# A four-layer graph network: the dilation's comparison on 2-byte operands in pairs of batches

## The chip, the cores and the metric

The kernel runs on one core of a Trainium2 chip. The metric is the device time of one execution in microseconds; the time of a kernel is the median of several executions. The engines are named as in the profile: PE is the matrix engine (PEld its weight loads), DVE the vector engine, ACT the scalar engine, POOL the GpSimd engine, SP the sync engine, which here only issues DMAs. `L1096` is line 1096 of the kernel before. The kernel is written against a layer that takes tiles and operations, inserts all waits, and orders each engine's instructions with a scheduler; each engine then executes its own instructions in that order.

## The reference

There are 16 batches of a graph of 1024 nodes with 128 features, and an adjacency matrix `adj` per batch, symmetric, of zeros and ones, with about 6% ones and a full diagonal. Four layers follow, each as `x = layernorm(x + layer(x, adj))`: an attention layer with a gate (0), a three-step neighbour aggregation on a *dilated* adjacency (1), a second attention layer with three gates (2), and a graph convolution (3). The change concerns the dilation alone, which comes ahead of layer 1:

```python
def step(carry, n):                       # n = 0 .. 1023, one row after the other
    row = jnp.take(carry, n, axis=0)
    nbi = row.astype(jnp.int32)
    num = jnp.sum(nbi)
    sf = jnp.where(num > T_DIL, (num + K_DIL - 1) // K_DIL, 1)   # T_DIL = 10, K_DIL = 2
    rank = jnp.cumsum(nbi)
    rm = row & (rank % sf == 0)
    valid = (mask_b[n] != 0) & (num > 1)
    rm = jnp.where(valid, rm, False)
    keep = ~rm
    carry = carry.at[n].set(row & keep)
    carry = carry.at[:, n].set(carry[:, n] & keep)
    return (carry, None)
...
adj_d = adj * jax.vmap(_dilate_pattern)(adj > 0, mask)
```

Each row loses the neighbours whose rank is a multiple of half of the row's count (that is, about the middle one and the last one), and the same entries are taken out of the column. Later rows see the removals of earlier ones.

## The kernel before, in words

The adjacency of all 16 batches lies in SBUF as FP8, in tiles `carry` (in the code `Y[b]`, 128 partitions by 8 blocks by 1024). Layer 0 fills them. Then comes the dilation, then layer 1, which reads the dilated matrices, and last a joint section for layers 2 and 3, which reads the undilated ones back from DRAM.

The dilation works on blocks of 128 rows (`k` = 0 to 7) and on two groups `g` of eight batches (`GB` = 8). A pair (k, g) is called a step here; there are 16, numbered 0 to 15 in the order k first, then g. One step has three parts.

`prepare` computes, for the 128 rows of the block, the rank of each member inside the diagonal block by matmuls against triangular matrices (L1068), once for each four batches (`QB` = 4). DVE masks the block (`uY`, L1062), multiplies ranks and mask into `sk` (L1070: 128 partitions by 8 batches by 128 members, fp16), and derives per row the count of members (`l1`, L1071) and a check (`past`, L1074). In the last two blocks (k = 6 and 7) it also marks the last member (`last`, L1076).

`fixed_point` finds which members of the diagonal block fall out. A row's middle rank depends on how many members earlier rows of the same block have taken from it, and so the kernel iterates: from a guess `ti` (128x8, int32) a threshold `thr` is made by setting the lowest bit (L1091); in blocks 6 and 7 also `even` (L1094); then `mid` = (`sk` == `thr`) over 128x1024 elements (L1096, FP8 result), whose ones are the middle members; PE counts them per row with eight matmuls, one for each batch, with a batch's 128x128 part of `mid` as weights and a column of ones as the moving operand (`pd`, L1099; in blocks 6 and 7 eight more with `last`, L1101); and DVE adds the count to the base `v1m` to give the next `ti` (L1103). Each turn of this loop is called an evaluation. Their number is fixed per block:

```python
EVALS = 2, 3, 4, 7, 7, 3, 3, 9
```

The last `mid` of a step is removed from the block's FP8 bits by XOR on 32-bit words (L1112), after `last` was added to it in blocks 6 and 7 (L1108, L1109). Then some ten small operations on 128x8 elements give the three values that the removals need: `negc`, `posc` and, as the last one, `wid` (L1129).

`removal` does the rest of the rows' width, one batch at a time. PE makes ranks of all 1024 columns (`s`, L1141 and L1143), ACT turns them into distances from the middle (`q`, L1144, two halves), DVE compares the distance with `wid` (`keep`, L1147) and masks the rows (L1148), PE transposes the result and adds it (`pc`, L1151 to L1155), and ACT writes the block's column (`carry`, L1156). In the last block each finished batch of the first half is also stored to DRAM (L1158).

The steps are woven as follows. Loop i (1 to 16) takes in turns the fixed point of step i and the eight removals of step i-1, and after each four removals one half of the `prepare` of step i+1. So a removal of step i waits for the `wid` of step i, and a fixed point waits for its own `prepare`, which reads what the removals before it left. The turns are only the order in which the program is written down; the scheduler orders the instructions of each engine from there. Ahead of loop 1, the fixed point of step 0 runs beside the end of layer 0 for the last batch, and a power on POOL (`deg`, L1187) is placed there too.

The tiles `sk`, `mid`, `uY`, `q` and `keep` have two buffers each.

Of the kernel before, what the change touches and what calls it, by code (L numbers as in the profile page):

```python
# [10 lines left out]
F16 = mybir.dt.float16  # L11
F32R = mybir.dt.float32r
BF16 = mybir.dt.bfloat16
I32 = mybir.dt.int32
I8 = mybir.dt.int8
FP8 = mybir.dt.float8e4
AF = mybir.ActivationFunctionType
OP = mybir.AluOpType
# [4 lines left out]
P = 128  # L23
# [4 lines left out]
EVALS = 2, 3, 4, 7, 7, 3, 3, 9  # L28
GB = 8
QB = 4  # L30
# [3 lines left out]
def general_kernel(ctx: ExitStack, tc: tile.TileContext, t: dict, out: bass.AP):  # L34
# [155 lines left out]
    with tc.tile_pool(name="m_sb", bufs=1) as sb, tc.tile_pool(name="m_ps", bufs=1, space=PSUM) as ps:  # L190
        mi = sb.tile([BT, P], I32, name="mi")
        nc.sync.dma_start(mi, t["nodemask"].rearrange("b (t p) -> (b t) p", p=P))
# [10 lines left out]
    carry_pool = carry_ctx.enter_context(tc.tile_pool(name="carry", bufs=1))  # L203
    C = [carry_pool.tile([P, NT, N], I8, name=f"carry{b}") for b in range(B)]

# [82 lines left out]
    with ExitStack() as ph:  # L288
# [15 lines left out]
        dr = seq.tile([P, B, P], F16, name="dr")  # L304
        M = seq.tile([B, P], I32, name="M")
        Mf = seq.tile([B, P], F32, name="Mf")
        cnt = seq.tile([P, 2, B], F32, name="cnt")
        cr1 = seq.tile([P, B], F32, name="cr1")
        par = seq.tile([B, 1], I32, name="par")
        tt = seq.tile([B, 1], F32, name="tt")  # L310
# [4 lines left out]
        for k in range(NT):  # L315
# [55 lines left out]
            def col(name, dtype=F32):  # L371
                return small.tile([P, B], dtype, name=name)

            v, vi, pr, z, q4, qp, cc, bias, wid, nz, bin_ = (
                col("v"), col("vi", I32), col("pr", I32), col("z"), col("q4"), col("qp"), col("cc"),
                col("bias"), col("wid"), col("nz"), col("bin"))
# [263 lines left out]
def fast_kernel(ctx: ExitStack, tc: tile.TileContext, t: dict, out: bass.AP, flag: bass.AP):  # L640

    nc = tc.nc
# [193 lines left out]
    with tc.tile_pool(name="m_sb", bufs=1) as sb, tc.tile_pool(name="m_ps", bufs=1, space=PSUM) as ps:  # L836
        mi = sb.tile([BT, P], I32, name="mi")
        nc.sync.dma_start(mi, t["nodemask"].rearrange("b (t p) -> (b t) p", p=P))
# [26 lines left out]
    onec = consts.tile([P, 1], BF16, name="onec")  # L865
# [28 lines left out]
    with tc.tile_pool(name="l0_raw", bufs=1, side="right") as raw:  # L894
# [4 lines left out]
        p = ps_h.tile([P, P], F32, name="wtr", tag="h")  # L899
# [3 lines left out]
        p = ps_h.tile([P, P], F32, name="wtr", tag="h")  # L903
# [3 lines left out]
        p = ps_h.tile([P, 1], F32, name="wtr", tag="h")  # L907
# [126 lines left out]
    with ExitStack() as ph:  # L1034
        sb = ph.enter_context(tc.tile_pool(name="dl_sb", bufs=2, side="right", reuse_waits="tile"))
        tiny = ph.enter_context(tc.tile_pool(name="dl_small", bufs=2, side="right", reuse_waits="tile"))
# [4 lines left out]
        def words(v):  # L1041
            return v.bitcast(I32)

        def per_member(v):
            return v[:, :, None].to_broadcast([P, v.shape[1], P])

        def prepare(st, k, g):

            ks = slice(k * P, (k + 1) * P)
            st.with_last = k >= NT - 2  # L1050
            st.sk = sb.tile([P, GB, P], F16, name="sk")
            st.v1m = tiny.tile([P, GB], F32, name="v1m")
            st.l1 = tiny.tile([P, GB], F32, name="l1")
            if st.with_last:
                st.last = sb.tile([P, GB, P], FP8, name="last")
            for q in range(GB // QB):
                qs = slice(q * QB, q * QB + QB)
                b0 = g * GB + q * QB
                gs = slice(b0, b0 + QB)
                Yg = Yq[b0 // QB]  # L1060
                uY = sb.tile([P, QB, P], FP8, name="uY")
                nc.vector.tensor_tensor(words(uY), words(Yg[:, :, k, ks]),  # L1062
                                        words(upper8)[:, None, :].to_broadcast([P, QB, P // 4]), op=OP.bitwise_and)
                s0 = ps_b.tile([P, QB, P], F32, name="s0")
                for i in range(QB):
                    for kb in range(NT):
                        m = step0 if kb == k else twos[:, :P if kb < k else 1]
                        nc.tensor.matmul(s0[:, i, :m.shape[1]], Y[b0 + i][:, kb, ks], m, start=(kb == 0), stop=(kb == NT - 1))  # L1068
                l1 = st.l1[:, qs]
                nc.vector.tensor_tensor(st.sk[:, qs, :], s0, uY, op=OP.mult)  # L1070
                nc.vector.scalar_tensor_tensor(l1, s0[:, :, 0], -1.0, off[:, k, gs], op0=OP.add, op1=OP.add)  # L1071
                if not st.with_last:

                    nc.vector.tensor_tensor(past[:, k, gs], l1, s0[:, :, P - 1], op=OP.subtract)  # L1074
                if st.with_last:
                    nc.vector.tensor_tensor(st.last[:, qs, :], st.sk[:, qs, :], per_member(l1), op=OP.is_equal, saturate=False)  # L1076
                yield

        def fixed_point(st, k, g):

            ks = slice(k * P, (k + 1) * P)
            gs = slice(g * GB, (g + 1) * GB)
            st.negc = negc = tiny.tile([P, GB], F32, name="negc")
            st.wid = wid = tiny.tile([P, GB], F32, name="wid")
            v1m, l1 = st.v1m, st.l1
            nc.vector.tensor_scalar(v1m, l1, 0.5, -0.5, op0=OP.mult, op1=OP.add)
            ti = tiny.tile([P, GB], I32, name="ti")
            nc.vector.tensor_copy(ti, v1m)
            for e in range(EVALS[k]):
                thr = tiny.tile([P, GB], I32, name="thr")  # L1090
                nc.vector.tensor_scalar(thr, ti, 1, None, op0=OP.bitwise_or)  # L1091
                if st.with_last:
                    even = tiny.tile([P, GB], BF16, name="even")
                    nc.vector.tensor_tensor(even, thr, ti, op=OP.is_equal)  # L1094
                mid = sb.tile([P, GB, P], FP8, name="mid")
                nc.vector.tensor_tensor(mid, st.sk, per_member(thr), op=OP.is_equal, saturate=False)  # L1096
                pd = ps_d.tile([P, GB], F32, name="pd")
                for i in range(GB):
                    nc.tensor.matmul(pd[:, i:i + 1], mid[:, i, :], onec, start=True, stop=not st.with_last)  # L1099
                    if st.with_last:  # L1100
                        nc.tensor.matmul(pd[:, i:i + 1], st.last[:, i, :], even[:, i:i + 1], start=False, stop=True)  # L1101
                tn = tiny.tile([P, GB], I32, name="ti")
                nc.vector.tensor_tensor(tn, pd, v1m, op=OP.add)  # L1103
                prev, ti = ti, tn
                yield
            nc.vector.tensor_tensor(bad[:, 0, k, gs], ti, prev, op=OP.not_equal)
            if st.with_last:
                nc.vector.tensor_tensor(st.last, st.last, per_member(even), op=OP.mult, saturate=False)  # L1108
                nc.vector.tensor_tensor(words(mid), words(mid), words(st.last), op=OP.bitwise_or)  # L1109
            for q in range(GB // QB):  # L1110
                yw = words(Yq[g * GB // QB + q][:, :, k, ks])
                nc.vector.tensor_tensor(yw, yw, words(mid[:, q * QB:(q + 1) * QB]), op=OP.bitwise_xor)  # L1112


            v = tiny.tile([P, GB], F32, name="v")
            nc.vector.tensor_sub(v, l1, ti)
            hw = tiny.tile([P, GB], F32, name="hw")
            nc.vector.tensor_tensor(hw, thr, prev, op=OP.is_equal)
            nc.vector.tensor_sub(negc, hw, v)
            nc.vector.scalar_tensor_tensor(hw, v, 0.5, hw, op0=OP.mult, op1=OP.mult)  # L1120
            nc.vector.tensor_sub(negc, negc, hw)
            st.posc = posc = tiny.tile([P, GB], F32, name="posc")
            nc.vector.scalar_tensor_tensor(posc, v, 2.0, negc, op0=OP.mult, op1=OP.add)
            en = tiny.tile([P, GB], F32, name="en")
            mk = mok[:, g * GB * NT + k:(g + 1) * GB * NT:NT]
            nc.vector.scalar_tensor_tensor(en, v, 10.5, mk, op0=OP.is_gt, op1=OP.mult)
            nc.vector.tensor_tensor(bad[:, 1, k, gs], en, mk, op=OP.not_equal)
            nc.vector.scalar_tensor_tensor(hw, hw, 1.0, en, op0=OP.add, op1=OP.mult)
            nc.vector.tensor_scalar(wid, hw, -1.0, None, op0=OP.add)  # L1129
            yield  # L1130
# [29 lines left out]
        def removals(now, then):  # L1160

            start = prepare(*then) if then else None
            for i in range(GB):
                removal(*now, i)
                yield
                if then and i % QB == QB - 1:
                    next(start)
                    yield
# [713 lines left out]
```

## Time and profile before

| what | value |
|---|---|
| median of 3 executions | 2661.71 us (2660.23 to 2662.22) |
| the profiled execution | 2657.81 us, its span 2656.1 us |
| granted PE clock in it, mean | 0.984 |
| layer 0 | 0 to about 611 us |
| prologue of the dilation | about 611 to 638 us |
| dilation, loops 1 to 16 | 638 to 990 us |
| layer 1, then layers 2 and 3 | from 990 us; the last stretch from about 1660 us |
| the comparison `mid` (L1096) | 76 times, 1.218 us at the median, from 622.0 to 963.8 us |

The profile gives, for each instruction, its engine, its source line, its tiles, its start and its duration. A stretch of time can be summed up by engine: a row then has the stretch, its length, the busy time of each engine with the count of instructions, the granted clock of PE as a fraction, the share of time in which the DMA engines were busy, and GB/s. Idle time in front of an instruction is put down to what released it. Durations on PE and DVE overlap a little, since the next instruction starts before the one before has been written down as ended: an operation that is listed with 1.22 us is followed by the next one after 1.14 us.

### The profile page before, as it was taken

Reading aid. Unit: us, or ns where it says so; the run is one execution under the profiler, and the core shown is the slowest. Engines: PE = TensorE matmul, PEld = TensorE weight load, DVE = VectorE, ACT = ScalarE, POOL = GpSimd, SP = SyncE. Lnnn points to the kernel's source line nnn. Section 1 sums busy time; section 2 is a strip of 40 time slices with the busy share of each in tenths; the row PEclk is TensorE's granted clock in tenths of the full one; section 3 lists DMA queues with packets and bytes.
Section 4 is the critical chain, followed back from the end, with each engine's and each line's share of the span. In section 5 each row is a group of like instructions: output and inputs, shape, how many; then the busy total and the mean of one; then the engine's idle time right before and its main releaser. Section 6 shows DMA issues by size and latency. Waiting matters only on the chain.

```text
span 2656.1 us, 44982 instructions
## 1 busy us (share of the span) xinstructions
PE 2509.0 (94%) x16580; PEld 1838.7 (69%) x16584; DVE 2106.4 (79%) x5832; ACT 1957.0 (74%) x3141; POOL 356.3 (13%) x316
## 2 busy tenths in 40 slices
PE   7999999997888869999999998999999999999987
PEld 5777777675666648888888896566666666666655
DVE  5888888887899877777788875777888787887786
ACT  7898898886888866667656534777777777777774
POOL 0001111013000001111122133011111111111001
PEclk9999999998999989999999998999999999999998
DMA  5555555530000052224467582111222111111100
GB/s 195 177 171 176 167 167 183 168 113 21 2 3 2 2 214 96 96 96 146 156 241 249 198 291 105 40 48 65 74 87 70 64 64 64 64 64 64 48 25 26
DMA packets 110103, 285.72 MB, mean 108 GB/s; under 512 B 12080, under 2 KB 53168, under 8 KB 102704
## 3 DMA queue, kind: packets, MB, share of 16 engines
q1 hardware_dynamic: 88832, 197.17, 22.1%
q0 software_dynamic: 21040, 85.57, 9.1%
q8 instruction: 133, 2.18, 0.3%
q14 instruction: 98, 0.80, 0.1%
HBM read 202.85 MB, written 79.82 MB: 106 GB/s over the span
## 4 chain that ended last, share of the span: by engine, by line
PE 53%; DVE 19%; ACT 13%; issue 5%; POOL 4%; DMA 2%; POOLq 0%; ACTq 0%; DVEq 0%; SPq 0%
PE acc L1306 9%; PE ph L1628 8%; PE acc L1694 6%; PE ph L1440 5%; PE ph L759 3%; PE ph L1644 3%; PE acc L973 2%; PE pmm L1706 2%; PE pmm L724 2%; PE ph L1615 2%; ACT em L985 2%; PE ph L766 2%; ACT xn L801 2%; DVE mid L1096 2%; DVE keep L1147 2%
## 5 line engine op out<-in xcount | busy, mean ns | idle before, releaser
L973 PEld LDWEIGHTS acc<-hs,em 128*128 128x128 f32 x2048 | 250.2, 193 | 38.2 <-issue 27.0
L973 PE MATMUL acc<-hs,em 128*128 128x128 f32 x2048 | 270.6, 280 | 0.9 <-DVE hs L989 0.7
L1694 PE MATMUL acc<-ex,hs 128*128 128x512 f32 x512 | 250.3, 599 | 6.2 <-DVE hs L1721 4.1
L724 PE MATMUL pmm<-xT,G 128*128 128x512 f32 x512 | 251.4, 604 | 1.4 <-DVE mx L983 0.7
L801 ACT ACTIVATE xn<-xn,ln_nb,ln_rstd 128x128 f32<-128x128 f32 x512 | 204.8, 480 | 55.3 <-DVE ln_nb L799 55.3
L1306 PE MATMUL acc<-a,hi 128*128 128x512 f32 x768 | 235.0, 398 | 3.0 <-ACT hi L1272 3.0
L1306 PE MATMUL acc<-a,lo 128*128 128x512 f32 x768 | 228.3, 392 | 3.1 <-DVE lo L1273 3.1
L745 POOL TENSOR_TENSOR ln_rstd<-ln_rstd,mhalf 128x8 f32<-128x8 f32 (+1 forms) x69 | 107.9, 1564 | 806.1 <-DVE ln_rstd L742 452.2
L1714 ACT ACTIVATE ex<-em,mn 128x1024 f32<-128x1024 f32 x128 | 146.6, 1145 | 89.2 <-DVE mn L1711 85.9
L983 DVE CUSTOM_DVE_ANT_0 em<-pmm,msk 128x1024 f32<-128x1024 f32 x128 | 155.9, 1218 | 35.5 <-PE pmm L724 33.2
L985 ACT ACTIVATE em<-em,mx 128x1024 f32<-128x1024 f32 x128 | 146.0, 1141 | 48.0 <-DVE mx L983 46.4
L1706 PE MATMUL pmm<-G,hT 128*128 128x512 f32 (+3 forms) x416 | 171.4, 520 | 0.1
L1306 PEld LDWEIGHTS acc<-a,lo 128*128 128x128 f32 x768 | 142.9, 188 | 34.0 <-DVE lo L1273 4.5
L1306 PEld LDWEIGHTS acc<-a,hi 128*128 128x128 f32 x768 | 140.7, 188 | 33.6 <-ACT hi L1272 3.7
L1156 ACT ACTIVATE carry<-pc,negone 128x1024 fp8e4<-128x1024 f32 x128 | 141.4, 1116 | 27.0 <-PE pc L1155 24.3
L1711 DVE CUSTOM_DVE_ANT_0 em<-pmm,msk 128x1024 f32<-128x1024 f32 x128 | 155.2, 1213 | 2.3 <-PE pmm L1708 0.6
L931 ACT ACTIVATE carry<-an 128x1024 fp8e4<-128x1024 f32 x128 | 134.1, 1049 | 24.5 <-DMA an<-in_adj 23.7
L980 ACT ACTIVATE msk<-carry,l0nbig 128x1024 bf16<-128x1024 fp8e4 x128 | 145.9, 1139 | 0.0
L1702 ACT ACTIVATE msk<-A,nbig 128x1024 bf16<-128x1024 fp8e4 x128 | 144.1, 1136 | 0.0
L1628 PE MATMUL ph<-A,hi 128*128 128x512 f32 x512 | 143.7, 422 | 0.2 <-ACT hi L1618 0.2
L1694 PEld LDWEIGHTS acc<-ex,hs 128*128 128x128 f32 x512 | 87.4, 189 | 78.6 <-issue 52.8
L1295 ACT CAST a<-carry 128x1024 fp32r<-128x1024 fp8e4 x96 | 98.9, 1047 | 43.4 <-PE acc L1306 43.2
(315 smaller groups left out, 6214.0 us busy)
## 6 DMA issues: line engine op xcount, KB each, us to landing
an<-in_adj SPq DMA_DIRECT2D x128, 512.0 KB, 4.1
adj_d<-carry POOLq DMA_DIRECT2D x16, 1024.0 KB, 4.6
A<-dil_d SPq DMA_DIRECT2D x16, 1024.0 KB, 6.0
rdeg<-rdeg_d SPq DMA_DIRECT2D x32, 512.0 KB, 4.6
A<-adj_d SPq DMA_DIRECT2D x16, 1024.0 KB, 4.8
ag_d<-ag POOLq DMA_DIRECT2D x24, 512.0 KB, 5.7
ag<-ag_d SPq DMA_DIRECT2D x24, 512.0 KB, 5.8
x_d<-xn POOLq DMA_DIRECT2D x16, 512.0 KB, 3.9
```

Source lines behind the costliest of these rows:

```text
L724: nc.tensor.matmul(p[:, h * 512:(h + 1) * 512], lhsT, rhs[:, h * 512:(h + 1) * 512], start=True, stop=True)
L801: nc.scalar.activation(r[:, k.start + i, :], r[:, k.start + i, :], AF.Identity, scale=rstd[:, i:i + 1], bias=nb[:, i:i + 1])
L973: nc.tensor.matmul(s.acc[:, c], em[:, c], hs, start=(jt == 0 and k % 4 == 0), stop=(jt == NT - 1 and k % 4 == 3))
L980: nc.scalar.activation(msk, Y[b][:, jt, :], AF.Identity, scale=-BIG, bias=nbig)
L983: nc.vector.tensor_tensor_reduce(em, e, msk, 1.0, 3.0e38, op0=OP.add, op1=OP.min, accum_out=mn)
L985: nc.scalar.activation(em, em, AF.Exp, scale=-1.0, bias=mn, accum_out=sm)
L1306: nc.tensor.matmul(acc, part[:, jt, :], pieces[h * NT // 2 + k][:, jt - 2 * k, :], start=(part is parts[0] and jt == 0), stop=(part is par ...
L1628: nc.tensor.matmul(p, part[:, jt, :], A[jt][:, c], start=(jt == 0 and i == 0), stop=(jt == NT - 1 and i == 1))
L1694: nc.tensor.matmul(s.acc[:, c], hs, ex[:, c], start=(jt == 0), stop=(jt == NT - 1))
L1706: nc.tensor.matmul(e[:, c], s.hT[:, js], s.G[:, c], start=True, stop=True)
L1711: nc.vector.tensor_tensor_reduce(row, e, msk, 1.0, 0.0, op0=OP.add, op1=OP.min, accum_out=mn)
L1714: nc.scalar.activation(ex, row, AF.Exp, scale=-1.0, bias=mn, accum_out=sm)
```

## The change

The tile `sk` is laid out in pairs of batches: 4 pairs by 128 members by 2 batches, so that the two batches of a pair lie next to each other, and two members of one batch are 4 bytes apart. `ti` and `thr` become 16-bit integers. In all evaluations of a step but the last, the result goes to a new tile `pairs` (bf16, the same layout as `sk`, two buffers), compared with the threshold's pair repeated over the members; the weights of the eight counting matmuls are then the bf16 members of one batch, 4 bytes apart. In the last evaluation of a step the result is still `mid` in FP8 and in the order of batches, read from `sk` across the pairs; `mid` has one buffer. The product that makes `sk` writes across the pairs, and `last` reads across them. The layouts of `s0`, `uY`, `last` and `carry` are unchanged.

```diff
+        def in_pairs(v):
+            return v.rearrange("p (a c) d -> p a c d", c=2)
+
+        def members(v):
+            return v.rearrange("p a d c -> p a c d")
...
-            st.sk = sb.tile([P, GB, P], F16, name="sk")
+            st.sk = sb.tile([P, GB // 2, P, 2], F16, name="sk")
...
-                nc.vector.tensor_tensor(st.sk[:, qs, :], s0, uY, op=OP.mult)
+                sk = members(st.sk[:, q * QB // 2:(q + 1) * QB // 2])
+                nc.vector.tensor_tensor(sk, in_pairs(s0), in_pairs(uY), op=OP.mult)
...
-                    nc.vector.tensor_tensor(st.last[:, qs, :], st.sk[:, qs, :], per_member(l1), op=OP.is_equal, saturate=False)
+                    nc.vector.tensor_tensor(in_pairs(st.last[:, qs, :]), sk, in_pairs(per_member(l1)), op=OP.is_equal, saturate=False)
...
-            ti = tiny.tile([P, GB], I32, name="ti")
+            ti = tiny.tile([P, GB], I16, name="ti")
             nc.vector.tensor_copy(ti, v1m)
             for e in range(EVALS[k]):
-                thr = tiny.tile([P, GB], I32, name="thr")
+                ends = e == EVALS[k] - 1
+                thr = tiny.tile([P, GB], I16, name="thr")
                 nc.vector.tensor_scalar(thr, ti, 1, None, op0=OP.bitwise_or)
...
-                mid = sb.tile([P, GB, P], FP8, name="mid")
-                nc.vector.tensor_tensor(mid, st.sk, per_member(thr), op=OP.is_equal, saturate=False)
+                if ends:
+                    mid = sb.tile([P, GB, P], FP8, name="mid", bufs=1)
+                    nc.vector.tensor_tensor(in_pairs(mid), members(st.sk), in_pairs(per_member(thr)), op=OP.is_equal, saturate=False)
+                    picked = [mid[:, i, :] for i in range(GB)]
+                else:
+                    pairs = sb.tile([P, GB // 2, P, 2], BF16, name="pairs")
+                    nc.vector.tensor_tensor(pairs, st.sk, thr.rearrange("p (a c) -> p a c", c=2)[:, :, None, :].to_broadcast([P, GB // 2, P, 2]),
+                                            op=OP.is_equal)
+                    picked = [pairs[:, i // 2, :, i % 2] for i in range(GB)]
                 pd = ps_d.tile([P, GB], F32, name="pd")
                 for i in range(GB):
-                    nc.tensor.matmul(pd[:, i:i + 1], mid[:, i, :], onec, start=True, stop=not st.with_last)
+                    nc.tensor.matmul(pd[:, i:i + 1], picked[i], onec, start=True, stop=not st.with_last)
...
-                tn = tiny.tile([P, GB], I32, name="ti")
+                tn = tiny.tile([P, GB], I16, name="ti")
```

More of the change, by code (lines that the diff above doesn't have):

```diff
@@ L14 @@
 I32 = mybir.dt.int32
+I16 = mybir.dt.int16
 I8 = mybir.dt.int8
```

## The prediction, made before the changed kernel ran

> **What bounds the kernel now.** I read the busy row of the page first, then a table of busy time by stretches that I cut at the ends of the dilation's removal loops, then the rows of the tile `mid`, and last the order of time on DVE at the end of the dilation. Over the whole span no engine is full all the time:
>
> ```profile
> PE 2509.0 (94%) x16580; PEld 1838.7 (69%) x16584; DVE 2106.4 (79%) x5832; ACT 1957.0 (74%) x3141; POOL 356.3 (13%) x316
> ```
>
> The comparison runs only between 622 and 965 us, so only the dilation counts (about 612 to 990 us). The columns below are: stretch, length, then busy us of PE, PEld, DVE, ACT, POOL, the granted clock, DMA. Each of the first six rows is one loop (675 to 695 is loop 3, 736 to 823 are loops 6 to 9, one by one); 909 to 941 is the fixed point of step 14 with the removals of step 13, and 941 to 969 that of step 15 with the removals of step 14.
>
> ```profile
> 675.46:695.44 19.98, 17.66 (x231) 12.85 (x229) 16.21 (x48) 18.04 (x25) 0.00 (x0) 1.00 0.01 2
> 736.53:757.92 21.39, 18.39 (x258) 13.44 (x256) 20.42 (x52) 17.11 (x23) 0.00 (x0) 1.00 0.01 2
> 757.92:779.86 21.94, 20.04 (x267) 14.30 (x264) 21.42 (x63) 18.24 (x25) 0.00 (x0) 1.00 0.02 5
> 779.86:801.70 21.84, 19.13 (x262) 13.99 (x259) 21.27 (x62) 18.06 (x24) 0.00 (x0) 1.00 0.01 2
> 801.70:823.44 21.74, 19.08 (x262) 14.16 (x259) 21.35 (x63) 18.60 (x25) 0.00 (x0) 1.00 0.01 2
> 909.03:940.89 31.86, 22.57 (x344) 17.12 (x343) 29.59 (x83) 19.47 (x25) 0.00 (x0) 0.85 0.01 2
> 940.89:968.68 27.79, 20.11 (x279) 14.26 (x277) 23.72 (x67) 17.59 (x24) 4.32 (x8) 0.87 0.74 301
> ```
>
> Three regimes are to be seen. Loop 3 has 3 evaluations and takes 20.0 us; ACT is busy for 18.0 of it and DVE for only 16.2. There ACT is the one waited for:
>
> ```profile
> DVE keep L1147 <- ACT q L1144: 8.0, 8, 2.9
> ```
>
> (the waits between 656 and 720 us). That is the floor of a loop: eight removals with 2 x 0.689 + 1.116 us of ACT each cannot go much faster. Loops 6 to 9 have 7 evaluations, take 21.4 to 21.9 us, and DVE is busy for all but 0.4 to 1.0 us: DVE is the bound. The last two stretches have 9 evaluations and ACT is busy for less than two thirds: there the chain of evaluations itself is the bound, since the removals of a step wait for its `wid`. The chain, in order of time on DVE, without a removal between:
>
> ```profile
> 932.53 1.22 DVE L1096 TENSOR_TENSOR mid<-sk,thr 128x1024 fp8e4<-128x1024 f16 x1
> ...
> 934.43 0.17 DVE L1103 TENSOR_TENSOR ti<-pd,v1m 128x8 int32<-128x8 f32 x1 [0.60 <-PE pd L1101]
> 934.63 0.17 DVE L1091 TENSOR_SCALAR thr<-ti 128x8 int32<-128x8 int32 x1
> 934.84 0.17 DVE L1094 TENSOR_TENSOR even<-thr,ti 128x8 bf16<-128x8 int32 x1
> 934.92 1.22 DVE L1096 TENSOR_TENSOR mid<-sk,thr 128x1024 fp8e4<-128x1024 f16 x1
> ```
>
> One turn is 2.39 us, half of it the comparison. The prologue (to 638 us) is held by POOL's 20.4 us power of `deg` (L1187), so its two evaluations gain nothing.
>
> **The change, part by part.** *The comparison.* 76 comparisons at 1.218 us; 60 become 2-byte (the number of evaluations less one, summed over 16 steps), 16 stay:
>
> ```profile
> L1099 PEld LDWEIGHTS <-mid x608: 95/95/147, 623.3 to 965.4; 128*128 128x128 fp8e4 x152
> L1096 DVE TENSOR_TENSOR mid<-sk,thr x76: 1214/1218/1227, 622.0 to 963.8; 128x1024 fp8e4<-128x1024 f16 x76
> ```
>
> No 2-byte two-input operation is in the trace. The nearest row is the product that makes `sk`, also a TENSOR_TENSOR, with half the elements, one per beat:
>
> ```profile
> L1070 DVE TENSOR_TENSOR sk<-s,uY 128x512 f16<-128x512 f32 x28 | 19.2, 686 | 8.6 <-PE s L1068 8.6
> ```
>
> From 1218 at 1024 and 686 at 512 elements, an element costs 1.04 ns and the rest is 154 ns. Two elements per beat thus give about 0.685 us, 0.533 less. That it engages I take from the Trainium skill, "Vector Engine (DVE) Microarchitecture Reference", section 5.1: a two-input operation takes two per beat if all three operands are 2-byte with innermost step 1 and more than one element there. Here `sk` and `pairs` are single runs, and the threshold's innermost pair (step 1, count 2) repeats, which the section also reports as fast. No row here shows it; the other end is 1.218, no gain.
>
> *Where 0.533 us counts.* Loops 7 to 9: DVE busy 21.3 less 6 x 0.533 = 18.1 us, under the floor. The 4-evaluation loops 4 and 5 together take 41.1 us with DVE at 34.8 (17.4 each), so DVE at 18 does not reach 20.0. I take 20.6 for loops 6 to 9: 86.9 - 82.4 = 4.5 us. Loops 4 and 5, with three cheap comparisons each: 0.8. Loops 12 and 13 (45.2 us, 2.6 each above the floor, two cheap comparisons each and further work for `last`): 1.5. Loops 2, 3, 10, 11 stand at 20.0 to 20.2: 0.3. The chain of step 14: eight cheap comparisons, 8 x 0.533 = 4.3. The chain of step 15: 4.3 too, but then its turns fall to about 2.5 us, and every turn now has one removal in it (the order of DVE's instructions in the changed program shows one `keep` between each two comparisons there), which ACT delivers every 2.5 us; I take 3.7. Sum: 4.5 + 0.8 + 1.5 + 0.3 + 4.3 + 3.7 = 15.1 us.
>
> *Thresholds in 16 bits* (`ti`, `thr`: 128x8): 0.16 us at 4 bytes, fixed cost; bounded by 0 and -0.01 us each, I take 0. *`mid` with one buffer*: it is now written once per step, and its reader, the XOR L1112, is over a whole chain before; without that cover it would be one wait per step. *3 KB more of SBUF per partition*: 0.
>
> *The 2-byte accesses 4 bytes apart*: `sk` is written so (32 times), `last` and the last comparison read it so (8 and 16 times). The trace has no such row. From below it is 0 against 0.686, 0.683 and 1.218. From above, the same reference, section 5.2: a stream that leaves a line at every element takes 1.71 to 1.76 ns per column for 1.05, so an estimated 0.35 us more per `sk` or `last` and 0.7 per last comparison, 1.4 us per loop. But the 4-byte words touched are adjacent, where the section reports full rate, so I take 0.
>
> *Weight loads.* 480 loads of `mid` become loads of 2-byte weights 4 bytes apart. Between starts of such pairs of load and matmul are now 27 ns:
>
> ```profile
> 933.85 0.17 PE L1101 MATMUL pd<-even,last 128*128 128x1 bf16 x1
> 933.88 0.17 PE L1099 MATMUL pd<-onec,mid 128*128 128x1 bf16 x1
> ...
> L1151 PEld LDWEIGHTS <-identb 128*128 128x128 bf16 x128 | 12.5, 98 | 7.5 <-DVE carry L1148 2.2 <-issue 1.4
> L1440 PEld LDWEIGHTS ph<-Wx,hT 128*128 128x128 f32 x640 | 99.4, 192 | 3.3 <-ACT nT L1478 0.4
> ```
>
> A contiguous 2-byte load takes 98 ns, as an FP8 one. A rule speaks against the change here: the skill's "TensorE: Matmul & The Clock Gate", section "Weight-path perf modes", says that fast loading reads 32 bits at a time, 4 FP8 or 2 bf16. Read that way, weights 4 bytes apart come one per read, four times 27 = 107 ns a pair, 0.64 us more per evaluation (8 pairs), and the 0.533 is gone: the sum would be about -1 us in place of -15. The rows show no dependence on the width (98 for 96), and the same section allows a step between columns; I take 0 and keep the 0.64, and the f32 row's 192 for 96 (0.78 per evaluation), for the range.
>
> *Moved instructions.* The scheduler's order changes only inside the dilation and the first batches after it. On POOL `rdeg_d` of the first batch goes ahead of the second batch's `d` (0.5 us of issue earlier); on SP one load of `A` goes behind three of `n`, but belongs to a batch some 200 us later; on ACT one copy `a` (L1295, 1.03 us) leaves the last loop and stands ahead of the first `hi`, where PE waited 2.6 us for ACT: what the last loop gains, that wait loses. Together 0, within 2 us either way.
>
> The profiled execution took 2657.8 us around its span of 2656.1, 3.9 under the median 2661.7; less 15.1 it would be 2642.7, and beside the median 2646.6.
>
> **The rivals.** *Strided weights load slowly* (slower): place L1099; price 0.64 to 0.78 us per evaluation; it decides from 0.533 / 8 = 67 ns per load on. With 0.78 the 16 cheap turns of the tail cost 16 x 0.25 = 4 us, and in loops 6 to 9 PE gets 4.7 us more beside 19 to 20 busy, near 24 us a loop, 2 more than now: 8 us; loops 4 and 5 about 2. Sum +14: 2676. For it: no strided 2-byte load exists now. Against it: the width rows. *Two per beat doesn't engage*: the comparison stays 1.22, time 2662, within 3; against it stands the rule, for it nothing but that f16, int16 and bf16 are mixed. *The gain is taken back by the order or by the strided streams*: DVE stops in order at a `keep` whose `q` is late, evaluations queue behind it, and 4 to 8 us remain: 2656. For it: the 8.0 us of waits at `keep` where DVE isn't full; against it: in the tail ACT has 10 to 12 us to spare.
>
> **How the numbers follow.** My forecast, 2647, own range 2640 to 2655: 0.62. Gain mostly taken back, 2656: 0.15, two thirds of it still faster by over 0.2% (5.3 us, about what a measurement of this kernel can tell from no change). No engagement: 0.09, nearly all within. Slow weights: 0.14, nearly all slower. So faster 0.62 + 0.10 = 0.72, same 0.05 + 0.08 + 0.01 = 0.14, slower 0.14. The range 2638 to 2663 leaves out the slow weights and a few hundredths below.
>
> **What would show it.** Right: the comparison to `pairs` near 0.685 us, its weight loads near 96 ns with 27 ns between pairs, loops 6 to 9 near 20.6 us with DVE near 18, the stretches 909 to 969 shorter by 8 us, `sk` still 0.69. Wrong: a comparison at 1.2 us (rule), pairs over 67 ns apart (weights), `sk` near 1.0 or the last comparison near 1.9 (streams), or idle time of DVE before `keep` in loops 6 to 9 that eats the 3.2 us (order).

## The result, and the profile after

| kernel | median, us | range | runs |
|---|---|---|---|
| before | 2661.41 | 2657.59 to 2664.31 | 6 |
| after | 2638.09 | 2636.29 to 2644.37 | 6 |

The ratio is 0.9916, with a 95% interval of 0.9907 to 0.9926: 23.3 us less, where the forecast had 15.1. The profiled execution of after took 2644.37 us, its span 2642.6; it was the longest of the six. Its dilation starts 3.6 us later than that of before (the first column write of `carry` at 641.92 against 638.33 us), in layer 0, which the edit does not touch. So the two traces are compared from the end of loop 1 to the end of loop 16, where the end of a loop is the start of its last column write: 334.4 us before (655.49 to 989.85), 312.7 after (659.17 to 971.90). That is 21.6 us less, and lies within the dilation. Kernels of the experiments below with the same order repeat both lengths: 335.3 and 334.8 us with the instructions as in before, 311.1 and 310.9 as in after. What follows the dilation took 4.5 us longer in the trace of after (1670.7 for 1666.2 us); over all the traces of this case that part varies from 1666 to 1673 us, so nothing is read from it.

The busy row of the page hardly moves; DVE is relieved of 27 us over the whole span:

```profile
PE 2512.8 (95%) x16584; PEld 1841.3 (70%) x16584; DVE 2079.4 (79%) x5832; ACT 1954.5 (74%) x3141; POOL 355.6 (13%) x316
```

The busy time by stretches (columns as in the prediction), for the same parts of the work: loop 3, loops 6 to 9 one by one, the fixed point of step 14, and that of step 15.

```profile
678.31:697.46 19.15, 17.21 (x231) 12.82 (x229) 15.26 (x48) 17.73 (x25) 0.00 (x0) 1.00 0.01 2
737.48:757.36 19.88, 18.09 (x259) 13.28 (x257) 18.36 (x61) 16.79 (x23) 0.00 (x0) 1.00 0.01 3
757.36:778.22 20.86, 19.10 (x260) 14.22 (x259) 18.61 (x62) 18.81 (x26) 0.00 (x0) 1.00 0.01 4
778.22:798.14 19.92, 18.31 (x256) 13.75 (x255) 18.58 (x61) 17.32 (x24) 0.00 (x0) 1.00 0.01 2
798.14:818.90 20.76, 18.92 (x256) 14.11 (x256) 18.71 (x60) 18.29 (x25) 0.00 (x0) 1.00 0.01 2
901.34:926.65 25.31, 22.32 (x348) 17.07 (x346) 24.62 (x79) 19.35 (x26) 0.00 (x0) 0.96 0.01 2
926.65:950.95 24.30, 20.33 (x279) 14.03 (x279) 20.89 (x70) 17.76 (x24) 4.32 (x8) 0.85 0.69 276
```

Loop 3 fell from 19.98 to 19.15, loops 6 to 9 from 86.9 to 81.4 together, and DVE there from 84.5 busy to 74.3. Step 14's stretch lost 6.6 us, step 15's 3.5. In loops 2 and 3 the waits of DVE for `q` add to 4.8 us before (655.49 to 695.44 us); after (659.17 to 697.46 us) they are the same, though the two loops are 1.7 us shorter:

```profile
DVE keep L1165 <- ACT q L1162: 4.9, 6, 1.2
```

The operations, as the rows of the tiles `pairs` and `sk` have them (minimum, median and maximum in ns):

```profile
L1117 PEld LDWEIGHTS <-pairs x480: 96/97/147, 626.4 to 945.0; 128*128 128x128 bf16 x160
...
L1112 DVE TENSOR_TENSOR pairs<-sk,thr x60: 682/685/693, 625.7 to 943.9; 128x1024 bf16<-128x1024 f16 x60
L1080 DVE TENSOR_TENSOR sk<-s,uY x32: 721/730/740, 619.5 to 922.5; 128x512 f16<-128x512 f32 x32
L1108 DVE TENSOR_TENSOR mid<-sk,thr x16: 1218/1222/1226, 628.6 to 946.1; 128x1024 fp8e4<-128x1024 f16 x16
L1086 DVE TENSOR_TENSOR last<-sk,l x8: 683/686/692, 852.0 to 925.8; 128x512 fp8e4<-128x512 f16 x8
```

The cheap comparison takes the 0.685 us of the estimate. The loads of 2-byte weights 4 bytes apart take 97 ns, 96 or less with 1-byte ones. Reading `sk` across the pairs costs at most 4 ns at the median (1222 for 1218, 686 for 683); writing it costs 44 ns (730 for 686).

One turn of the chain of step 14, in order of time on DVE:

```profile
906.53 0.69 DVE L1112 TENSOR_TENSOR pairs<-sk,thr 128x1024 bf16<-128x1024 f16 x1
907.13 0.75 DVE L1165 TENSOR_SCALAR keep<-q,wid 128x1024 fp8e4<-128x1024 f16 x1
907.86 0.17 DVE L1121 TENSOR_TENSOR ti<-pd,v1m 128x8 int16<-128x8 f32 x1
907.95 0.42 DVE L1166 TENSOR_TENSOR carry<-carry,keep 128x256 int32<-128x256 int32 x1
908.28 0.17 DVE L1102 TENSOR_SCALAR thr<-ti 128x8 int16<-128x8 int16 x1
908.48 0.16 DVE L1105 TENSOR_TENSOR even<-thr,ti 128x8 bf16<-128x8 int16 x1
908.56 0.69 DVE L1112 TENSOR_TENSOR pairs<-sk,thr 128x1024 bf16<-128x1024 f16 x1
```

A turn takes 2.03 us and holds a whole `keep`, which lies where DVE would otherwise wait for PE's counts. In the trace of before the eight turns of this chain took 2.36 to 3.40 us: 2.39 with no `keep` in it, 2.56 with one, 3.36 and 3.40 with two (the turns that begin at 920.59 and 923.95 us). From the first comparison to the ninth it was 22.3 us, and 16.8 after. So more changed here than 0.533 us: the scheduler, which was given a shorter comparison, also wrote another order. The experiments ask what each of the two is worth.

### The profile page after: what moved, and what is told of

Same layout as the page of the kernel before. It is cut to its first block, busy times and chain, and to the rows that moved or that the text cites. A ratio compares the mean times of both kernels' runs of the same rounds, so it can differ in the third digit from the quotient of the medians.

```text
span 2642.6 us, 44971 instructions
## 1 busy us (share of the span) xinstructions
PE 2512.8 (95%) x16584; PEld 1841.3 (70%) x16584; DVE 2079.4 (79%) x5832; ACT 1954.5 (74%) x3141; POOL 355.6 (13%) x316
## 4 chain that ended last, share of the span: by engine, by line
PE 55%; DVE 18%; ACT 14%; issue 5%; POOL 4%; DMA 2%; POOLq 0%; ACTq 0%; DVEq 0%; SPq 0%
PE acc L1324 10%; PE ph L1646 8%; PE acc L1712 6%; PE ph L1458 5%; PE ph L760 3%; PE ph L1662 3%; PE acc L974 3%; PE pmm L725 3%; PE pmm L1724 2%; PE ph L1633 2%; ACT em L986 2%; PE ph L767 2%; ACT xn L802 2%; DMA an<-in_adj 2%; POOL ln_rstd L746 2%
```

## The experiments

The theory: the time comes from the comparison's 0.533 us, through DVE in loops 6 to 9 and through the chain in the tail; the order and the strided accesses count for little. (The tail is the chains of steps 14 and 15.) Its rival: the order that the scheduler writes decides, and the shorter comparison is only its occasion.

**Four-byte thresholds.** All of the change but the 2-byte thresholds; the instructions then stand in the order of before.

```diff
-            ti = tiny.tile([P, GB], I16, name="ti")
+            ti = tiny.tile([P, GB], I32, name="ti")
...
-                thr = tiny.tile([P, GB], I16, name="thr")
+                thr = tiny.tile([P, GB], I32, name="thr")
...
-                tn = tiny.tile([P, GB], I16, name="ti")
+                tn = tiny.tile([P, GB], I32, name="ti")
```

> The changed kernel with one thing undone: ti and thr are 32-bit again, so that one of the comparison's three operands is 4 bytes wide; the pairs of batches, the bf16 result and the strided weights stay. DVE's order of comparisons and keeps falls back to that of the kernel before. If the gain comes from two elements per beat, the comparison to pairs takes 1.22 us again and the time is 2662 us, within 3 (what the layout costs by itself: 44 ns on each of 32 products sk, about 1 us). If the gain came from the layout or the weights, the comparison would be shorter than 1.1 us or the time under 2655.

Measured 2663.0 us (ratio to before 1.0004, interval 0.9995 to 1.0013). The row of the comparison:

```profile
L1112 DVE TENSOR_TENSOR pairs<-sk,thr x60: 1212/1218/1226, 621.9 to 964.9; 128x1024 bf16<-128x1024 f16 x60
```

One 4-byte operand among the three, though it has only 8 elements per partition, is enough to lose all. Layout, strided weights and the additional buffer together then cost nothing that can be told.

**An FP8 result.** The cheap comparison with all of the change except that `pairs` is FP8.

```diff
-                    pairs = sb.tile([P, GB // 2, P, 2], BF16, name="pairs")
+                    pairs = sb.tile([P, GB // 2, P, 2], FP8, name="pairs")
...
-                                            op=OP.is_equal)
+                                            op=OP.is_equal, saturate=False)
```

> The changed kernel with pairs in FP8 instead of bf16 (weights 2 bytes apart, thresholds 16-bit): the result alone is 1 byte wide. If all three operands must be 2 bytes wide, the comparison takes 1.22 us; if the two inputs decide, 0.69. Weight loads 96 ns in either case. Time about 2661 or about 2638.

```profile
L1112 DVE TENSOR_TENSOR pairs<-sk,thr x60: 1211/1218/1226, 623.5 to 963.6; 128x1024 fp8e4<-128x1024 f16 x60
```

One run took 2666.31 us. The 1-byte result loses all as well; so the result must be 2-byte, and PE's weights with it.

**The old order of comparisons and keeps, with the fast comparison; and the new order with the slow one.** The 76 comparisons and 128 keeps are chained by edges that order two instructions of one engine and add no wait; the rest is left to the scheduler. The first kernel is the changed one with the sequence of before; the second has 4-byte thresholds and the sequence of after.

```diff
+        line = [next(left[c]).ins for c in ORDER]        # "MMKKMMKKKK...": M a comparison, K a keep
+        for first, then in zip(line, line[1:]):
+            tc.add_manual_dep(then, first.name, mybir.DependencyInfo(mybir.DependencyClass.NoSync, mybir.DependencyReason.DATA), ...)
```

> The changed kernel (comparison at 0.685 us), but with DVE's order of the 76 comparisons and 128 keeps fixed to that of the kernel before. If the comparison's 0.533 us is all and the forecast missed only the order's share, the time is 2646 us (15 us gained, as forecast). If the order matters little, 2638 to 2640. If the two only work together (a turn of the chain needs one keep behind each comparison), 2650 or more.

> As the kernel with 32-bit thresholds (comparison at 1.22 us), but with DVE's order of the 76 comparisons and 128 keeps fixed to that of the changed kernel. If the order alone makes up what the forecast missed (7 us), the time is 2654 to 2656, and the stretch from the end of loop 13 to the wid of step 14 falls from 31.9 to about 29 us. If the order is worth something only with short comparisons, it stays at 2659 to 2664.

Fast comparison, old sequence: 2661.23 us, ratio 0.9999 (0.9990 to 1.0008), with the comparison at 0.684. Slow comparison, new sequence: 2664.46, ratio 1.0010 (1.0001 to 1.0019). Neither alone gains. Where the first one loses it is seen in loop 8, in order of time on DVE:

```profile
783.32 0.17 DVE L1107 TENSOR_SCALAR thr<-ti 128x8 int16<-128x8 int16 x1
783.96 0.75 DVE L1170 TENSOR_SCALAR keep<-q,wid 128x1024 fp8e4<-128x1024 f16 x1 [0.47 <-ACT q L1167]
784.75 0.42 DVE L1171 TENSOR_TENSOR carry<-carry,keep 128x256 int32<-128x256 int32 x1
786.12 0.75 DVE L1170 TENSOR_SCALAR keep<-q,wid 128x1024 fp8e4<-128x1024 f16 x1 [0.94 <-ACT q L1167]
786.79 0.68 DVE L1117 TENSOR_TENSOR pairs<-sk,thr 128x1024 bf16<-128x1024 f16 x1
```

The threshold is ready at 783.5, but two keeps stand ahead of its comparison, and DVE waits for the `q` of each; the comparison starts 3.3 us late. In before the same two keeps (786.62 and 787.82 us) cost no wait: DVE was behind, and their `q` lay ready. Over the dilation the waits at `keep` grew to 47.8 us, from 30.4.

But this held only one of the engines' orders, and PE's differed from that of both kernels. So:

**The whole order of the dilation.** The same edges chain all 5268 instructions of the dilation, 4000 on PE, 884 on DVE and 384 on ACT. First the changed kernel in the order of before, then the one with 4-byte thresholds in the order of after.

```diff
+        for engine, text in ORDERS.items():               # PE, DVE, ACT: places of the other kernel's order
+            line = [made[engine][int(n)].ins for n in text.split()]
+            for first, then in zip(line, line[1:]):
+                tc.add_manual_dep(then, first.name, ...)
```

> The changed kernel with the 0.685 us comparison, but all 5268 instructions of the dilation on PE, DVE and ACT (4000, 884 and 384) follow each other in the order that they have in the kernel before; edges that add no wait. With only comparisons and keeps held in the old order the gain was gone (2661). If the order of the whole stage is needed for the gain, this is 2655 to 2663, with DVE idle before keep in loops 7 to 9 and in the tail. If that earlier null came from PE or ACT being rearranged around a half-held order, the old order as a whole lets the 0.533 us through: 2646 or below. Comparison 0.685 us in both cases.

> The kernel with 4-byte thresholds (comparison 1.218 us), but all instructions of the dilation on PE, DVE and ACT in the order of the changed kernel. If order and duration only work together: 2660 to 2668 (holding only comparisons and keeps gave 2664). If the new order as a whole, with PE's part, is worth something by itself: 2650 to 2657.

With these the four corners are there (medians in us; each ratio is to the runs of before beside it, with its interval):

| | comparison 1.22 us | comparison 0.685 us |
|---|---|---|
| order of before | 2661.41 | 2655.17: 0.9973 (0.9966 to 0.9981) |
| order of after | 2669.68: 1.0026 (1.0017 to 1.0035) | 2638.09: 0.9916 (0.9907 to 0.9926) |

For the two new kernels the runs of before beside them have a median of 2662.31. So the faster comparison alone is worth 7 us, the order alone costs 7 us, and both together gain 23. From the end of loop 1 to the end of loop 16 the traces say much the same (7.1 gained, 9.3 lost, 21.6 gained): 334.4 us in before, 327.3 with the fast comparison in the old order, 343.7 with the slow one in the new order, 312.7 in after. Of the changed kernel in the old order, the stretches (loops 7 and 8, loops 6 to 9 together, then the fixed points of steps 14 and 15):

```profile
758.04:779.48 21.44, 19.39 (x267) 14.43 (x264) 18.56 (x63) 18.04 (x25) 0.00 (x0) 1.00 0.02 5
779.48:800.85 21.37, 18.60 (x262) 14.14 (x259) 18.43 (x62) 18.05 (x25) 0.00 (x0) 1.00 0.01 2
737.68:822.14 84.46, 74.48 (x1031) 56.50 (x1028) 73.44 (x235) 71.35 (x96) 0.00 (x0) 1.00 0.01 3
907.08:936.44 29.36, 21.70 (x344) 16.99 (x342) 25.27 (x83) 18.94 (x25) 0.00 (x0) 0.90 0.01 2
936.44:963.09 26.65, 20.29 (x279) 14.67 (x279) 20.39 (x66) 17.98 (x24) 4.32 (x8) 0.82 0.73 295
```

and what DVE waits for in loops 6 to 9 (us in total, times, longest):

```profile
DVE ti L1126 <- PE pd L1122: 7.2, 11, 1.2
DVE keep L1170 <- ACT q L1167: 1.6, 5, 0.4
```

In loops 6 to 9 DVE is busy for 73.4 us, 11.0 less than before and about as in after, but the loops are only 2.5 us shorter than before: most of the freed time has become idle time, and the largest part of it is a wait for the counts on PE. Over the whole dilation DVE's waits for counts grew from 6.9 us to 19.0, those at `keep` from 30.4 to 36.4. From the `wid` of step 13 to that of step 15 it is 65.2 us, 68.9 before and 57.0 after. Why the counts are late is seen in one turn of step 14, first DVE, then PE:

```profile
918.28 0.68 DVE L1117 TENSOR_TENSOR pairs<-sk,thr 128x1024 bf16<-128x1024 f16 x1
918.88 0.75 DVE L1170 TENSOR_SCALAR keep<-q,wid 128x1024 fp8e4<-128x1024 f16 x1
920.42 0.17 DVE L1126 TENSOR_TENSOR ti<-pd,v1m 128x8 int16<-128x8 f32 x1 [0.79 <-PE pd L1124]
```

```profile
918.45 0.70 PE L1166 MATMUL s<-step,carry 128*128 128x512 bf16 x4
918.99 0.33 PE L1082 MATMUL s<-step,carry 128*128 128x128 bf16 x3
919.35 0.65 PE L1164 MATMUL s<-step,carry 128*128 128x512 bf16 x3
919.84 0.17 PE L1122 MATMUL pd<-onec,pairs 128*128 128x1 bf16 x1
```

The comparison has ended at about 918.9, but on PE three groups of matmuls of a removal and of `prepare` stand ahead of its counts, which begin at 919.84. From comparison to `ti` it is 2.14 us. The same turn of before:

```profile
920.59 1.22 DVE L1096 TENSOR_TENSOR mid<-sk,thr 128x1024 fp8e4<-128x1024 f16 x1
922.72 0.17 DVE L1103 TENSOR_TENSOR ti<-pd,v1m 128x8 int32<-128x8 f32 x1 [0.25 <-PE pd L1101]
```

```profile
920.76 0.70 PE L1143 MATMUL s<-step,carry 128*128 128x512 bf16 x4
921.30 0.33 PE L1068 MATMUL s<-step,carry 128*128 128x128 bf16 x3
921.66 0.65 PE L1141 MATMUL s<-step,carry 128*128 128x512 bf16 x3
922.14 0.17 PE L1099 MATMUL pd<-onec,mid 128*128 128x1 bf16 x1
```

It has the same three groups on PE and takes 2.13 us. Nothing is gained in this turn, because that order had filled a 1.2 us comparison with work for PE. In after, PE has less work in that place of the turn shown above:

```profile
906.88 0.54 PE L1159 MATMUL s<-step,carry 128*128 128x512 bf16 x2
907.27 0.18 PE L1117 MATMUL pd<-onec,pairs 128*128 128x1 bf16 x1
```

Counts begin 0.74 us after the comparison's start, `ti` 1.33 us after it.

The other corner is the mirror image: with the slow comparison in the new order PE stands still at the counts. In loops 6 to 9, 93.9 us long there, its row of waits is

```profile
PE pd L1122 <- DVE pairs L1117: 10.1, 23, 0.9
```

against 1.5 us in before (for `mid`, L1096). PE's matmuls behind those counts, the removals' `s` among them, come late, and so does ACT's `q`: it waits 11.3 us for `s` in these loops, 2.8 before. What the edges that hold an order cost by themselves was not measured; the turn above, 2.14 us with them and 2.13 without, shows no cost.

PE's granted clock differs between these traces too: in the stretch of step 14 it is 0.85 before, 0.90 with the fast comparison in the old order and 0.96 after. It does not decide the length there: the first kernel of the next experiment has 0.97 in that stretch, and takes 26.57 us for after's 25.31.

**The gain by blocks.** The cheap form in block 7 only (steps 14 and 15), and in blocks 3 and 4 only (steps 6 to 9); the order is the scheduler's own.

```diff
-                ends = e == EVALS[k] - 1
+                ends = e == EVALS[k] - 1 or k != 7               # the other kernel: k not in (3, 4)
```

> The changed kernel with the cheap comparison in block 7 alone (steps 14 and 15, 16 comparisons); all other evaluations use the 1.22 us form into mid. The scheduler orders it freely. If the gain of each part stands by itself: the tail's part of the trace, 10.3 us, so 2651; by the forecast's terms 4.3 + 3.7 = 8.0, 2653.5. If the scheduler needs the faster stage as a whole to find the good order, less: 2656 or above.

> The changed kernel with the cheap comparison in blocks 3 and 4 alone (steps 6 to 9, 24 comparisons). If the parts stand by themselves: 5.5 us by the trace (4.5 by the forecast), so 2656 to 2657, with loops 6 to 9 at 81 us together and the tail at 81 as before. If a gain here is lost again by another order later: 2660 or above.

Block 7: 2651.65 us against 2662.28, ratio 0.9958 (0.9942 to 0.9975): 10.6 us, close to the 10.3 that the tail of the trace said. From the `wid` of step 13 to that of step 15 it is 58.7 us. Blocks 3 and 4: 2655.54, ratio 0.9971 (0.9962 to 0.9980), 6.7 us; loops 6 to 9 take 81.4 us (739.06 to 820.44), the same as in after. The parts nearly add: 10.6 and 6.7 of 23.3, and the other 6.0 matches what loops 2 to 5, 12 and 13 lost in the trace (1.7 + 1.1 + 3.3). So the cheap form need not be everywhere for the scheduler to find a good order: each of the two parts tried gains by itself. The other blocks were not tried alone.

**The strided accesses.** In one kernel the weights of the cheap evaluations are 128 contiguous bf16 columns; in the other `sk` is written, and read by `last` and the last comparison, contiguously. Both leave out the right assignment of members to batches, and with it the right result.

```diff
+                    flat = pairs.rearrange("p a d c -> p (a d c)")
-                    picked = [pairs[:, i // 2, :, i % 2] for i in range(GB)]
+                    picked = [flat[:, i * P:(i + 1) * P] for i in range(GB)]
...
```

```diff
-                sk = members(st.sk[:, q * QB // 2:(q + 1) * QB // 2])
-                nc.vector.tensor_tensor(sk, in_pairs(s0), in_pairs(uY), op=OP.mult)
+                sk = in_order(st.sk)[:, qs, :]
+                nc.vector.tensor_tensor(sk, s0, uY, op=OP.mult)
...
```

> The changed kernel with the weights of the cheap evaluations read as 128 contiguous bf16 columns in place of 128 columns 4 bytes apart. Part changed: the counts are those of other members, so thresholds converge to other values; the flag that would enter the general kernel is multiplied by zero. If the strided 2-byte load costs nothing (97 ns against 96 to 98 of contiguous rows, pairs 27 ns apart): within 2 us of the changed kernel's 2638, loads 96 to 98 ns. If the stride does cost on PE and is only hidden in the record: 480 pairs get shorter, 2633 or below.

> The changed kernel with sk written contiguously by its product, and last and the last comparison reading it contiguously (as in the kernel before), while the cheap comparison still reads the same bytes as pairs. Part changed: members are compared with the threshold of another batch; the flag that would enter the general kernel is multiplied by zero. sk should fall from 730 back to about 686 ns (32 times 44 ns, 1.4 us in all), last and the last comparison stay at 0.68 and 1.22. If that is all: 2636.5 to 2638, since part of it is off the path. If the order that the scheduler finds changes as well, the time can move by more than 1.4 us either way.

```profile
L1118 PEld LDWEIGHTS <-pairs x480: 95/96/147, 622.0 to 942.0; 128*128 128x128 bf16 x160
```

```profile
L1083 DVE TENSOR_TENSOR sk<-s,uY x32: 681/691/693, 613.4 to 918.2; 128x512 f16<-128x512 f32 x32
```

Contiguous weights: 2639.32 us, ratio 0.9914 (0.9881 to 0.9947), loads of 96 ns for 97. Contiguous `sk`: 2640.68, ratio 0.9918 (0.9886 to 0.9951). With four runs each these intervals hold after's 0.9916, and no gain is seen. The stride on the weights costs nothing; the write across the pairs costs 39 ns at the product, 1.2 us over 32 of them, and what of it reaches the end is below what these runs can tell.

**The last evaluation too.** All evaluations in the cheap form, with `mid` made from the last `pairs` by a copy, on DVE or on POOL.

```diff
-                    nc.vector.tensor_tensor(in_pairs(mid), members(st.sk), in_pairs(per_member(thr)), op=OP.is_equal, saturate=False)
+                    nc.vector.tensor_copy(in_pairs(mid), members(pairs), saturate=False)      # the other kernel: nc.gpsimd
...
```

> The changed kernel, but the last evaluation of a step is compared in pairs too (0.685 us), and its FP8 mid is made from the pairs by a DVE copy beside PE's counts. By the nearest row, keep with 0.747 us at the same size, DVE has about 0.2 us more per step (3.4 us in all), while the last turn of a chain is 0.53 us shorter; that counts in steps 14 and 15 only. Expected 2636 to 2640 (no gain that can be told). If the copy stands ahead of the ti that ends the chain, 2640 to 2643.

> The same with the copy on POOL, which is idle in this stage. DVE is relieved of 0.53 us per step, and the XOR into carry waits for POOL instead. No row shows POOL at this size; up to about 1.3 us per copy it is hidden behind the last count and the ten small operations, then 2630 to 2637. If it takes 3 us or more, the XOR and with it the next prepare come late, or DVE is slowed beside it: 2640 or above.

```profile
L1112 DVE CAST mid<-pairs x16: 684/687/695, 627.2 to 947.3; 128x1024 fp8e4<-128x1024 bf16 x16
```

With the copy on DVE: 2643.66 us, ratio 0.9926 (0.9909 to 0.9943), not better than after and just above both expectations. Loops 2 to 6 are 3.3 us shorter than after's (94.9 for 98.2, a loop of three evaluations 18.6), but loops 7 to 9 are 2.4 longer and the chain of step 15 1.5. With the copy on POOL: 2649.38, ratio 0.9946 (0.9929 to 0.9963), slower than after and than expected for a copy of this length. The row of the copy, DVE's wait for it, and POOL in order of time:

```profile
L1112 POOL CAST mid<-pairs x16: 1027/1102/1597, 635.4 to 957.0; 128x1024 fp8e4<-128x1024 bf16 x16
```

```profile
DVE carry L1128 <- POOL mid L1112: 8.7, 1, 8.7
```

```profile
614.69 20.74 POOL L1203 TENSOR_TENSOR deg<-deg,mhalf 128x128 f32<-128x128 f32 x1 [1.24 <-DVE deg L1202]
635.40 1.03 POOL L1112 CAST mid<-pairs 128x1024 fp8e4<-128x1024 bf16 x1
```

The copy itself fits (1.10 us, and DVE waits for it only once in the whole stage), but that one stands behind POOL's power in the prologue. From the start of the power to the first column write of `carry` it is 32.3 us here and 25.7 in after; without these 6.7 us the time would be an estimated 2643, still no better than after. A copy on DVE for the first step alone, or a later power, was not tried. So no version better than after came out.

## Why the prediction was right, point by point

The direction was right, and so was the cause as far as it went: the comparison took the time that was forecast, and without it there is no gain. That the number was right as well is luck: 2638.09 us lies 0.09 us inside the stated range of 2638 to 2663, and outside the forecast's own range of 2640 to 2655. The gain was half as large again as the sum, and the term behind that, the order of the instructions, stood in the sum at 0.

- **The comparison at 0.685 us: right.** The rule of the Trainium skill, "Vector Engine (DVE) Microarchitecture Reference", section 5.1, that all three operands must be 2-byte, is shown from both sides: 685 ns with bf16, f16 and int16 mixed and the threshold's pair repeated, 1218 with a 4-byte threshold, 1218 with an FP8 result.
- **Weight loads: right to go by the rows.** 97 ns at a stride of 4 bytes, 96 contiguous. The four times slower reading of "TensorE: Matmul & The Clock Gate", "Weight-path perf modes", is not borne out by this load, and contiguous weights gain nothing.
- **Strided streams: nearly right.** Reads 0, as taken. The write of `sk` was said to stay at 0.69 us; it is 0.73, much nearer to the 0 that was taken than to the 0.35 us more of the bound.
- **Thresholds, one `mid` buffer:** 0.164 us as before, and no wait at `mid`.
- **Loops 6 to 9: 5.5 us, forecast 4.5.** The step that was off is "the floor of a loop", 20.0 us, "cannot go much faster": loops 2 and 3 fell to 19.1, loops 6 and 8 to 19.9, and the kernel with the copy on DVE has loops of 18.6. The floor was a sum of listed durations, 8 x (2 x 0.689 + 1.116) = 19.95 us, and these overlap: the prediction's own row has ACT busy for 18.04 us in loop 3, 2.26 for each removal. The other 1.9 us were idle time, and 0.8 of them went, most only with the new order: with the fast comparison in the old order loops 2 and 3 take 19.9 and 19.6 us.
- **Loops 4 and 5: 1.1 us, forecast 0.8. Loops 2, 3, 10, 11: 1.5 against 0.3, all of it in loops 2 and 3. Loops 12 and 13: 3.3 against 1.5.** In loops 2 and 3 it is the same term. In loops 12 and 13 it is the order: with the fast comparison in the old order they lose only 0.6 us.
- **The chain of step 14: 6.6 us, forecast 4.3; of step 15: 3.5, forecast 3.7.** Step 14 gained more than eight times 0.533: its eight turns lost 5.5 us together, as each now holds at most one `keep`, where two had held two and others none. "ACT delivers every 2.5 us" is the same sum of listed durations, and was wrong: in the later turns of step 15 the keeps follow each other every 2.02 to 2.35 us. Also, in before the first comparison of step 15 (939.76, 1.2 us) stood ahead of the `wid` of step 14 (940.89), and in after it stands behind (927.23 and 926.65).
- **"Moved instructions ... Together 0, within 2 us": the step that failed in kind.** It looked at what enters and leaves the stage. Inside it the order is worth 16 us with the fast comparison (the 23.3 of both less the 7.1 of the comparison alone) and costs 7 with the slow one. The forecast's sum let 0.533 us pass straight through at every place; with the order of before only 7 of the 15 us pass: 2.5 in loops 6 to 9, 2.5 in the chain of step 14, 1.1 in that of step 15, 1.7 in other loops, less 0.7 in the last one. The new order was known when the forecast was made, and was used there for step 15 alone.
- **The rival "gain taken back by the order", 2656, is what the kernel in the old order does, at 2655.17,** though more by PE's order, with 7.2 us of waits for counts in loops 6 to 9, than by the `keep` it named, with 1.6. It did not come about, because the scheduler counts with the shorter comparison: with 4-byte thresholds, the only difference, it writes the order of before. The strided weights and the comparison without effect are both out.

The terms that were too small add to 6.5 us (1.0, 0.3, 1.2, 1.8 and 2.2), all of one sign; step 15's 0.2 too much is set off by the last loop, 0.2 shorter. That is the difference between the 15.1 of the sum and the 21.6 of the trace; the medians have another 1.7. Two slips of the prediction bear on nothing: five of its rows are single loops, not six, and a load decides against the gain when it is 67 ns longer, that is with pairs some 94 ns apart, not 67.

## What to carry to other kernels

A shorter instruction in a woven schedule is worth what the order lets through: here the same 0.533 us was worth 7 us in the old order and 23 in one written for it, and that order was a loss for the slow instruction. So when a duration changes, read both engines at the same turn: what stands on PE between the start of the operation and the first reader of its result had been fitted to the old duration. An engine's busy share in a loop that it seems to bound, 18.0 of 20.0 us, is no floor until no other order makes the loop shorter, and a sum of listed durations is none either where these overlap.

## What the runs showed of the hardware beyond that

- A write of 2-byte elements 4 bytes apart costs DVE 39 to 44 ns at 512 elements (730 for 686 to 691), while reads of that kind cost 3 to 4 ns at most.
- A DVE copy of 128x1024 from bf16 to FP8 across the pairs takes 687 ns; the same copy on POOL 1102 ns.
